# A decoder layer's FFN with its inner features on partitions from the first product on, and its layernorm taken through the second product from running sums

## The chip, the cores and the metric

The kernel runs on one core of a Trainium2 chip. The core has five engines with queues of their own: TensorE (PE in the profile; its weight loads, PEld, are listed apart), VectorE (DVE), ScalarE (ACT), GpSimd (POOL) and SyncE (SP, which here only issues DMAs). The metric is the device time of one execution in microseconds (us), of which several runs of a kernel are taken and the median is quoted.

## The reference

One pre-norm decoder layer over x of shape (4, 1024, 256): self-attention with 16 heads, cross-attention over 64 context tokens, and an FFN. Only the FFN is changed:

```python
m, v = mean(x, -1), var(x, -1)
xn = (x - m) / sqrt(v + 1e-5)                        # layernorm without weights, over 256
h = gelu(xn @ absmean(W_fc).T)                       # 256 -> 1024, exact gelu
mu, var = mean(h, -1), mean((h - mu) ** 2, -1)       # over the 1024 inner features
h = (h - mu) * rsqrt(var + 1e-5) * ln_w + ln_b
x = x + h @ absmean(W_proj).T                        # 1024 -> 256
```

absmean(W) turns a weight matrix into values of -1, 0 and 1. All data are float32.

## The kernel before

Tokens lie on partitions in tiles of 128; E = 256, HID = 1024, NT = 8 tiles to a batch, B = 4 batches. The long first stage (the loop `for u in range(NU)`, L891) runs the self-attention of all batches, and between its steps the projections and the rest (`post`, L540: output projection, cross-attention) of the batch before. The helper `fill` (L694) places that work; a third line of work, `aside`, takes the last batch's spare places for `ternary` (L722, absmean of the two weight matrices) and `bias_row` (L760). `bias_row` makes `yrow`, the row ln_b @ W_proj, on TensorE as plain float32, in the four 32-column strips that `product` uses in this stage.

After the loop the pools are closed and new ones opened (L962 to L971): PSUM as `wide`, two tiles of two banks each, and `misc`, four tiles of one bank each. What follows I call the last stage. It runs the FFN of all 32 token tiles, and beside it the generator `last`, which is `post` of batch 3.

The FFN works on eight halves of a batch (NH = 4 tiles, 512 tokens). `widen(i)` (L976) does for half i: `ln_normalised` and `ln_transposed` of two tiles at a time (four TensorE transposes into one bank; ACT casts to `xh`, DVE makes the rest `xl`, both in the float32r format), `add_row` of `yrow` on POOL (L280), then per tile 8 matmuls of 512 columns with weights `xl`/`xh` and moving `wfc` into a `wide` tile; the gelu over 1024 columns goes to `h` with the tokens on partitions (L1001), DVE takes its statistics (L1004, L1005). When all four tiles are there, `ln_rstd` takes a square root on ACT and a reciprocal on DVE, and `h` is normalised in place, two tiles on DVE (L1012), two on ACT (L1015).

`narrow(i)` (L1020) takes the 8 chunks of 128 inner features: four transposes of `h` into one `misc` bank, ACT scales by `lnw` and rounds to `hT` (L1035), DVE makes the rest `hl` (L1036), and two chunks later 8 matmuls of 256 columns add into `py`, a `wide` tile. At the end DVE adds `py` to x (L1052) and SP issues two stores.

PE instructions and the DMAs on SP keep the order in which the program issues them. The order of the last stage is written out by hand: `widen` and `narrow` of each half are generators with a place number for every step (`WIDE`, `NARROW`, L1077, 16 numbers to a half), the generator with the lowest next number steps, and two of every five turns go to `last` (L1085). `narrow(i)` begins only when `widen(i)` is done, and a step of gelus isn't taken while `last` is between its exponentials (L1095).

Of the kernel before, what the change touches and what calls it, by code (L numbers as in the profile page):

```python
# [10 lines left out]
F32R = mybir.dt.float32r  # L11
DRAM = bass.MemoryType.DRAM
# [8 lines left out]
HID = 1024  # L21
# [9 lines left out]
def decoder_layer(ctx, tc, a, out):  # L31
# [204 lines left out]
    def ln_rstd(pool, rs, mv):  # L236
        n = mv.shape[1]
        sd = pool.tile([P, n], F32, tag="sd", name="sd", bufs=2)
        nc.scalar.activation(sd, mv[:, :, 1], AF.Sqrt, bias=eps_t[:, 0:1])
        nc.vector.reciprocal(out=rs, in_=sd)  # L240

# [478 lines left out]
    yrow = const.tile([P, E], F32, name="yrow")  # L720

# [37 lines left out]

    def bias_row():  # L760

        yield "free"
        wide = main.tile([P, HID // P, P], F32, tag="hl", name="lnb_wide", bufs=2)
        nc.gpsimd.tensor_copy(
            wide, late["lnb"].rearrange("p (c o) -> p c o", o=1).to_broadcast([P, HID // P, P])
        )
        yield "cols"
        pt = bank()
        w = ternaries[1].bitcast(F32)
        product(pt[:, 0:E], [(wide[:, c, :], w[:, c, :]) for c in range(HID // P)])  # L770
        nc.vector.tensor_copy(yrow, pt[:, 0:E])
# [119 lines left out]
    for u in range(NU):  # L891
# [23 lines left out]
        if g == 1 and b == B - 1:  # L915
            aside.add(ternary("wfc", 2, HID), 10)
            aside.add(ternary("wproj", HID // P, E), 10)
            aside.add(bias_row(), 2)
# [54 lines left out]
    h_of = {}  # L973
    NH = NT // 2

    def widen(i):  # L976
# [10 lines left out]
        h = ffn.tile([P, NH, HID], F32, tag="h", name="h", bufs=2)  # L987
        mv = ffn.tile([P, NH, 2], F32, tag="mvh", name="mvh", bufs=2)
        rs = ffn.tile([P, NH], F32, tag="rsh", name="rsh", bufs=2)
        h_of[i] = h  # L990
        for t in range(NH):
            yield "Gelu"
            ph = ps["wide"]()
            for half in range(2):
                for k in range(4):
                    c, part = divmod(k, 2)
                    matmul(
                        ph[:, half, :], lhsT=(xl, xh)[part][:, c, t * P : (t + 1) * P],
                        rhs=wfc[:, c, half * 512 : (half + 1) * 512], start=k == 0, stop=k == 3,
                    )  # L1000
            nc.scalar.activation(h[:, t, :], ph.rearrange("p a f -> p (a f)"), AF.Gelu)  # L1001
            st = ffn.tile([P, 2, 6], F32, tag="bnh", name="bnh", bufs=3)
            for half in range(2):
                nc.vector.bn_stats(out=st[:, half, :], in_=h[:, t, half * 512 : (half + 1) * 512])  # L1004
            nc.vector.bn_aggr(out=mv[:, t, :], in_=st)  # L1005
        yield "Sqrt"
        ln_rstd(ffn, rs, mv)
        nmr = ffn.tile([P, NH], F32, tag="nmr", name="nmr", bufs=2)
        nc.vector.scalar_tensor_tensor(nmr, mv[:, :, 0], -1.0, rs, ALU.mult, ALU.mult)
        for t in range(0, NH, 2):  # L1010
            yield ""
            nc.vector.tensor_scalar(  # L1012
                h[:, t, :], h[:, t, :], mv[:, t, 0:1], rs[:, t : t + 1], ALU.subtract, ALU.mult
            )
            nc.scalar.activation(  # L1015
                h[:, t + 1, :], h[:, t + 1, :], AF.Identity, bias=nmr[:, t + 1 : t + 2],
                scale=rs[:, t + 1 : t + 2],
            )

    def narrow(i):  # L1020


        h = h_of.pop(i)
        t0 = i * NH
        py = ps["wide"]()
        parts = []
        for c in range(HID // P + 2):
            if c < HID // P:
                pt = bank()
                for n in range(NH):  # L1030
                    transpose(pt[:, n * P : (n + 1) * P], h[:, n, c * P : (c + 1) * P], ident)
                hT = ffn.tile([P, 512], F32R, tag="hT", name="hT", bufs=4)
                hl = ffn.tile([P, 512], F32R, tag="hl", name="hl", bufs=4)
                w = late["lnw"][:, c : c + 1]
                nc.scalar.activation(hT, pt, AF.Copy, scale=w)  # L1035
                nc.vector.scalar_tensor_tensor(hl, pt, w, hT.bitcast(F32), ALU.mult, ALU.subtract)  # L1036
# [127 lines left out]
```

## Time and profile before

Three runs gave 1364.13, 1367.08 and 1367.55 us, median 1367.08. The profiled execution took 1365.17 us, of which its span is 1363.4 us.

| stretch of the span | us | PE busy | DVE busy | ACT busy | POOL busy |
|---|---|---|---|---|---|
| to the end of the attention loop, 0 to 1101.6 | 1101.6 | 1048.7 | 834.9 | 741.0 | 53.9 |
| FFN with post of batch 3, 1101.6 to 1298.4 | 196.8 | 178.6 | 130.7 | 122.5 | 23.5 |
| FFN alone, one half to the next, 1298.4 to 1322.8 | 24.4 | 21.5 | 17.0 | 16.3 | 2.7 |
| to the end, 1322.8 to 1363.4 | 40.6 | 33.3 | 22.2 | 18.7 | 0.0 |

Busy times are from the profile's table by stretches. A busy PE is not a PE at its peak: the matmuls overlap, so what a group of them costs is read from one start to the next. The groups of instructions give for each line, engine and operation the output and inputs by the program's names, the shape, the count, the total and the mean in ns; "ps_misc<-ident,h" are the transposes of `h`, "ps_wide<-wfc,xl" matmuls of the first product, "ps_wide<-wproj,hl" of the second.

### The profile page before, as it was taken

How to read it: one execution, taken by the hardware profiler on the slowest of the kernel's cores; microseconds unless marked ns; L12 is line 12 of the kernel's file. 1: busy time of each engine (PE TensorE's matmuls, PEld its weight loads, DVE VectorE, ACT ScalarE, POOL GpSimd, SP SyncE). 2: the span in 40 equal slices, each digit the busy share in tenths (PEclk: the TensorE clock that was granted, in tenths of full speed). 3: DMA queues.
4: the chain of work that ended last, by engine and by line, in shares of the span. 5: the costliest groups of instructions: out<-in, count | busy, mean ns of one | idle time of the engine just before them, and what ended most of it. 6: DMA issues, size and time to landing. Idle time of an engine off the chain costs nothing.

```text
span 1363.4 us, 27651 instructions
## 1 busy us (share of the span) xinstructions
PE 1282.1 (94%) x11000; PEld 717.4 (53%) x11000; DVE 1004.7 (74%) x2110; ACT 898.5 (66%) x1654; POOL 80.0 (6%) x86
## 2 busy tenths in 40 slices
PE   3879999999999999999999999999999988999987
PEld 1434445545545454444545544545455466776777
DVE  4877777867878877877877777878889357565665
ACT  1377666756687667777676676676766746474765
POOL 4000000003010000011000000010000012000000
PEclk9889999999999999989999999999999989999989
DMA  5440312312130202131212112212210010100000
GB/s 169 126 143 30 111 42 68 94 48 63 41 85 1 63 7 57 33 93 31 64 35 60 38 27 75 82 53 73 55 40 1 2 62 1 44 19 31 1 31 32
DMA packets 46064, 72.72 MB, mean 53 GB/s; under 512 B 11280, under 2 KB 27920, under 8 KB 45936
## 3 DMA queue, kind: packets, MB, share of 16 engines
q1 hardware_dynamic: 44720, 68.47, 17.0%
q8 instruction: 87, 1.43, 0.4%
q10 hardware_dynamic: 1072, 2.10, 0.4%
q0 software_dynamic: 144, 0.39, 0.2%
q14 instruction: 41, 0.34, 0.1%
HBM read 46.81 MB, written 24.12 MB: 52 GB/s over the span
## 4 chain that ended last, share of the span: by engine, by line
PE 73%; DVE 16%; ACT 8%; issue 2%; DMA 1%; SPq 0%; DVEq 0%; ACTq 0%
PE ps_ring L57 42%; PE ps_acc L57 15%; PE ps_wide L57 8%; DVE mx L433 8%; PE ps_misc L57 3%; ACT exp L888 3%; PE ps_misc L60 2%; PE ps_ring L60 2%; DVE nm L592 2%; ACT xn L250 1%; DVE xn L256 1%; DVE bn L233 1%; DMA x<-in_x 1%; ACT ex L625 1%; ACT hl L359 1%
## 5 line engine op out<-in xcount | busy, mean ns | idle before, releaser
L433 DVE TENSOR_REDUCE mx<-ps_ring 128x1 f32<-128x512 f32 x1024 | 646.4, 682 | 157.6 <-PE ps_ring L57 156.7
L888 ACT ACTIVATE exp<-ps_ring 128x512 f32<-128x512 f32 x1024 | 549.2, 606 | 191.1 <-PE ps_ring L57 187.5
L57 PE MATMUL ps_ring<-q,k 64*128 64x512 f32 x1024 | 280.5, 474 | 8.0 <-ACT exp L888 5.9
L57 PE MATMUL ps_ring<-k,q 64*128 64x512 f32 x1024 | 260.2, 425 | 20.1 <-DMA q<-kept_q 7.9
L57 PE MATMUL ps_acc<-exp,v_sb 128*32 128x512 f32 x2048 | 275.3, 610 | 0.0
L57 PE MATMUL ps_ring<-mT,sel 64*128 64x512 f32 x1024 | 232.8, 400 | 0.2 <-ACT mT L451 0.2
L57 PEld LDWEIGHTS ps_ring<-q,k 64*128 64x128 f32 x1024 | 115.5, 185 | 198.4 <-ACT exp L888 69.0
L57 PEld LDWEIGHTS ps_ring<-k,q 64*128 64x128 f32 x1024 | 124.2, 186 | 100.2 <-ACT exp L888 41.3
L57 PEld LDWEIGHTS ps_ring<-mT,sel 64*128 64x128 f32 x1024 | 108.0, 186 | 6.3 <-ACT mT L451 0.7
L57 PEld LDWEIGHTS ps_acc<-exp,v_sb 128*32 128x32 f32 x2048 | 40.5, 108 | 67.4 <-issue 65.6
L1004 DVE BATCH_NORM_STATS2 bnh<-h 128x6 f32<-128x512 f32 x64 | 41.2, 679 | 34.1 <-ACT h L1001 34.0
L1001 ACT ACTIVATE h<-ps_wide 128x1024 f32<-128x1024 f32 x32 | 32.7, 1026 | 41.6 <-PE ps_wide L57 41.5
L1036 DVE SCALAR_TENSOR_TENSOR hl<-ps_misc,lnw,hT 128x512 fp32r<-128x512 f32 x64 | 46.4, 733 | 18.2 <-ACT hT L1035 18.2
L57 PE MATMUL ps_wide<-wproj,hl 128*128 128x256 f32 x256 | 46.2, 303 | 12.6 <-DVE hl L1036 12.5
L57 PE MATMUL ps_wide<-wfc,xl 128*128 128x512 f32 x128 | 56.5, 442 | 1.4 <-DVE xl L271 1.4
L57 PE MATMUL ps_wide<-wfc,xh 128*128 128x512 f32 x128 | 54.3, 424 | 0.0
L1035 ACT ACTIVATE hT<-ps_misc,lnw 128x512 fp32r<-128x512 f32 x64 | 42.6, 687 | 16.3 <-PE ps_misc L60 16.3
L233 DVE BATCH_NORM_STATS2 bn<-x 128x6 f32<-128x256 f32 x96 | 38.8, 416 | 8.1 <-DMA x<-in_x 6.4
L57 PEld LDWEIGHTS ps_wide<-wproj,hl 128*128 128x128 f32 x256 | 34.9, 191 | 16.2 <-DVE hl L1036 14.8
L280 POOL TENSOR_TENSOR x<-x,xbo 128x512 f32<-128x512 f32 x16 | 20.6, 1295 | 367.0 <-ACT xn L250 358.5
L57 PE MATMUL ps_wide<-wproj,hT 128*128 128x256 f32 x256 | 41.4, 284 | 0.0
L407 ACT COPY v_sb<-ps_ring 128x256 f32<-128x256 f32 x32 | 12.0, 375 | 41.0 <-PE ps_ring L57 30.6
(166 smaller groups left out, 1467.1 us busy)
## 6 DMA issues: line engine op xcount, KB each, us to landing
k<-kept_k SPq DMA_DIRECT2D x248, 64.0 KB
q<-kept_q SPq DMA_DIRECT2D x240, 64.0 KB
kept_q<-hl SPq DMA_DIRECT2D x15, 512.0 KB
kept_k<-hl SPq DMA_DIRECT2D x14, 512.0 KB
out<-x SPq DMA_DIRECT2D x16, 256.0 KB
x<-in_x SPq DMA_DIRECT2D x3, 1024.0 KB
x_kept<-x SPq DMA_DIRECT2D x3, 1024.0 KB
x<-x_kept SPq DMA_DIRECT2D x3, 1024.0 KB
```

Of the source, the lines that this page charges most:

```text
L57: ordered(nc.tensor.matmul(*args, **kwargs))
L60: ordered(nc.tensor.transpose(*args))
L233: nc.vector.bn_stats(out=st, in_=xs(t)[:, 0, :])
L250: nc.scalar.activation(xn[:, k, :], xs(t + k)[:, 0, :], AF.Identity, bias=nmr[:, k : k + 1], scale=rs[:, i + k : i + k + 1],)
L280: nc.gpsimd.tensor_tensor(xs(t, 2), xs(t, 2), row.rearrange("p (o d) -> p o d", o=1).to_broadcast([P, 2, E]), ALU.add,)
L433: nc.vector.tensor_reduce(mx[:, t, 2 * pair + n : 2 * pair + n + 1, kh], pm, AX.X, ALU.max)
L592: nc.vector.tensor_reduce(nm[:, t, s, :], pm[s].rearrange("p (h k) -> p h k", k=SK), AX.X, ALU.max, negate=True,)
L888: nc.scalar.activation(ex[:, n, :], pe[n], AF.Exp)
L1001: nc.scalar.activation(h[:, t, :], ph.rearrange("p a f -> p (a f)"), AF.Gelu)
L1004: nc.vector.bn_stats(out=st[:, half, :], in_=h[:, t, half * 512 : (half + 1) * 512])
L1035: nc.scalar.activation(hT, pt, AF.Copy, scale=w)
L1036: nc.vector.scalar_tensor_tensor(hl, pt, w, hT.bitcast(F32), ALU.mult, ALU.subtract)
```

## The change

The first product is turned round: `wfc` becomes the stationary operand and xh/xl the moving one, so that a PSUM bank holds 128 inner features of 512 tokens. Per chunk c of 8, ACT takes the gelu into `h`, scales `h` by `lnw` into `hT` and squares `h` into `sq`; DVE makes `hl` from `h` and `hT` and adds `h` to a running sum; POOL adds `sq` to a second running sum. The transposes of `h`, its statistics, its square root and its normalisation in place go.

After chunk 7 the two sums are transposed on TensorE (8 transposes), reduced on DVE to mean and mean square of each token, and POOL works out 1/sqrt(var + eps) by `ln_root`: a first value from the bits, three Newton steps. In these and the four operations ahead of it are 21 small POOL operations of 128x4.

The second product works on the h that is scaled by `lnw` but neither shifted nor normalised. `narrow` has no transposes; it adds to x, in steps c = 3 and 5, `crow` times -mean/std (`crow` is the row lnw @ W_proj), and at the end `py` times 1/std. `yrow` and `crow` are made at the start of the last stage, with 16 float32r matmuls each, whose stationary operand is a column of `lnb` or `lnw` repeated 128 times; `bias_row` goes from the attention loop.

The first product's banks come from `misc` now, `wide` serves `py` alone, `h` has four buffers of one chunk, `sq` three, `hT` and `hl` ten each. The places of the steps and the share of turns for `last` are new: 7 steps of `widen`, 8 of `narrow`, and four of every nine turns.

```diff
+    def ln_root(pool, rs, mv):
+        n = mv.shape[1]
+        by = pool.tile([P, 4, n], F32, tag="root", name="root", bufs=2)
+        var, half, t, nmr = (by[:, i, :] for i in range(4))
+        engine = nc.gpsimd
+        engine.tensor_scalar(var, mv[:, :, 1], 0.0, LN_EPS, ALU.max, ALU.add)
+        engine.tensor_scalar(half, var, -0.5, None, ALU.mult)
+        engine.tensor_scalar(
+            rs.bitcast(I32), var.bitcast(I32), -0.5, float(0x5F3759DF), ALU.mult, ALU.add
+        )
+        for _ in range(3):
+            engine.tensor_tensor(t, rs, half, ALU.mult)
+            engine.tensor_tensor(t, t, rs, ALU.mult)
+            engine.tensor_scalar(t, t, 1.5, None, ALU.add)
+            engine.tensor_tensor(rs, rs, t, ALU.mult)
+        engine.tensor_tensor(nmr, mv[:, :, 0], rs, ALU.mult)
+        engine.tensor_scalar(nmr, nmr, -1.0, None, ALU.mult)
+        return nmr
...
-            aside.add(bias_row(), 2)
...
-        h = ffn.tile([P, NH, HID], F32, tag="h", name="h", bufs=2)
+        h_of[i] = deque()
+        sums = ffn.tile([P, 2, 512], F32, tag="sums", name="sums", bufs=2)
+        last = None
+        for c in range(HID // P):
+            if c % 2 == 0:
+                yield "Gelu"
+            ph = bank()
+            for k in range(4):
+                f, part = divmod(k, 2)
+                matmul(
+                    ph, lhsT=wfc[:, f, c * P : (c + 1) * P], rhs=(xl, xh)[part][:, f, :],
+                    start=k == 0, stop=k == 3,
+                )
+            h = ffn.tile([P, 512], F32, tag="h", name="h", bufs=4)
+            sq = ffn.tile([P, 512], F32, tag="sq", name="sq", bufs=3)
+            hT, hl = (ffn.tile([P, 512], F32R, tag=tag, name=tag, bufs=10) for tag in ("hT", "hl"))
+            h_of[i].append((hl, hT))
+            nc.scalar.activation(h, ph, AF.Gelu)
+            w = late["lnw"][:, c : c + 1]
+            nc.scalar.activation(hT, h, AF.Copy, scale=w)
+            nc.scalar.activation(sq, h, AF.Square)
+            nc.vector.scalar_tensor_tensor(
+                hl, h, w, hT.bitcast(F32), ALU.mult, ALU.subtract
+            )
+            if last is not None:
+                before = last if c == 1 else (sums[:, 0, :], sums[:, 1, :])
+                nc.vector.tensor_tensor(sums[:, 0, :], before[0], h, ALU.add)
+                nc.gpsimd.tensor_tensor(sums[:, 1, :], before[1], sq, ALU.add)
+            last = h, sq
+        yield ""
         mv = ffn.tile([P, NH, 2], F32, tag="mvh", name="mvh", bufs=2)
         rs = ffn.tile([P, NH], F32, tag="rsh", name="rsh", bufs=2)
-        h_of[i] = h
-        for t in range(NH):
-            yield "Gelu"
-            ph = ps["wide"]()
-            for half in range(2):
-                for k in range(4):
-                    c, part = divmod(k, 2)
-                    matmul(
-                        ph[:, half, :], lhsT=(xl, xh)[part][:, c, t * P : (t + 1) * P],
-                        rhs=wfc[:, c, half * 512 : (half + 1) * 512], start=k == 0, stop=k == 3,
-                    )
-            nc.scalar.activation(h[:, t, :], ph.rearrange("p a f -> p (a f)"), AF.Gelu)
-            st = ffn.tile([P, 2, 6], F32, tag="bnh", name="bnh", bufs=3)
-            for half in range(2):
-                nc.vector.bn_stats(out=st[:, half, :], in_=h[:, t, half * 512 : (half + 1) * 512])
-            nc.vector.bn_aggr(out=mv[:, t, :], in_=st)
-        yield "Sqrt"
-        ln_rstd(ffn, rs, mv)
-        nmr = ffn.tile([P, NH], F32, tag="nmr", name="nmr", bufs=2)
-        nc.vector.scalar_tensor_tensor(nmr, mv[:, :, 0], -1.0, rs, ALU.mult, ALU.mult)
-        for t in range(0, NH, 2):
-            yield ""
-            nc.vector.tensor_scalar(
-                h[:, t, :], h[:, t, :], mv[:, t, 0:1], rs[:, t : t + 1], ALU.subtract, ALU.mult
-            )
-            nc.scalar.activation(
-                h[:, t + 1, :], h[:, t + 1, :], AF.Identity, bias=nmr[:, t + 1 : t + 2],
-                scale=rs[:, t + 1 : t + 2],
-            )
+        total = ffn.tile([P, 3, NH], F32, tag="total", name="total", bufs=2)
+        for k in range(2):
+            pt = bank()
+            for n in range(NH):
+                transpose(pt[:, n * P : (n + 1) * P], sums[:, k, n * P : (n + 1) * P], ident)
+            nc.vector.tensor_reduce(
+                total[:, k, :], pt.rearrange("p (n k) -> p n k", n=NH), AX.X, ALU.add
+            )
+        mean, square = mv[:, :, 0], total[:, 2, :]
+        nc.gpsimd.tensor_scalar(mean, total[:, 0, :], 1.0 / HID, None, ALU.mult)
+        nc.gpsimd.tensor_tensor(square, mean, mean, ALU.mult)
+        nc.gpsimd.tensor_scalar(mv[:, :, 1], total[:, 1, :], 1.0 / HID, None, ALU.mult)
+        nc.gpsimd.tensor_tensor(mv[:, :, 1], mv[:, :, 1], square, ALU.subtract)
+        shift_of[i] = rs, ln_root(ffn, rs, mv)
 
     def narrow(i):
-        h = h_of.pop(i)
+        parts = h_of.pop(i)
+        rs, nmr = shift_of.pop(i)
         t0 = i * NH
         py = ps["wide"]()
-        parts = []
-        for c in range(HID // P + 2):
-            if c < HID // P:
-                pt = bank()
+        for c in range(HID // P):
+            if c:
+                yield ""
+            for k, part in enumerate(parts.popleft()):
                 for n in range(NH):
-                    transpose(pt[:, n * P : (n + 1) * P], h[:, n, c * P : (c + 1) * P], ident)
-                hT = ffn.tile([P, 512], F32R, tag="hT", name="hT", bufs=4)
-                hl = ffn.tile([P, 512], F32R, tag="hl", name="hl", bufs=4)
-                w = late["lnw"][:, c : c + 1]
-                nc.scalar.activation(hT, pt, AF.Copy, scale=w)
-                nc.vector.scalar_tensor_tensor(hl, pt, w, hT.bitcast(F32), ALU.mult, ALU.subtract)
-                parts.append((hl, hT))
-            if c >= 2:
-                for k, part in enumerate(parts[c - 2]):
-                    for n in range(NH):
-                        matmul(
-                            py[:, n // 2, n % 2 * E : (n % 2 + 1) * E], lhsT=part[:, n * P : (n + 1) * P],
-                            rhs=wproj[:, c - 2, :], start=c == 2 and k == 0 and n % 2 == 0,
-                            stop=c == HID // P + 1 and k == 1 and n % 2 == 1,
-                        )
-            if 0 < c < HID // P + 1:
-                yield ""
-        for n in range(2):
-            rows = xs(t0 + 2 * n, 2)
-            nc.vector.tensor_tensor(
-                rows, rows, py[:, n, :].rearrange("p (n d) -> p n d", n=2), ALU.add
-            )
-            dma(out=out_view[:, t0 + 2 * n : t0 + 2 * n + 2, :], in_=rows)
+                    matmul(
+                        py[:, n // 2, n % 2 * E : (n % 2 + 1) * E],
+                        lhsT=part[:, n * P : (n + 1) * P], rhs=wproj[:, c, :],
+                        start=c == 0 and k == 0 and n % 2 == 0,
+                        stop=c == HID // P - 1 and k == 1 and n % 2 == 1,
+                    )
+            if c in (3, 5):
+                for n in range(c - 3, c - 1):
+                    row = xs(t0 + n)[:, 0, :]
+                    nc.vector.scalar_tensor_tensor(
+                        row, crow, nmr[:, n : n + 1], row, ALU.mult, ALU.add
+                    )
+        for n in range(NH):
+            row = xs(t0 + n)[:, 0, :]
+            nc.vector.scalar_tensor_tensor(
+                row, py[:, n // 2, n % 2 * E : (n % 2 + 1) * E], rs[:, n : n + 1], row, ALU.mult,
+                ALU.add,
+            )
+            if n % 2:
+                dma(out=out_view[:, t0 + n - 1 : t0 + n + 1, :], in_=xs(t0 + n - 1, 2))
         if i == 1:
             load_x(2, view=x_kept, slot=1)
+    yrow, crow = (ffn.tile([P, E], F32, name=name) for name in ("yrow", "crow"))
+    for row, name in ((yrow, "lnb"), (crow, "lnw")):
+        two = ffn.tile([P, 2, HID // P], F32R, name=f"{name}_parts")
+        nc.vector.tensor_copy(two[:, 0, :], late[name])
+        nc.vector.tensor_tensor(two[:, 1, :], late[name], two[:, 0, :].bitcast(F32), ALU.subtract)
+        pt = bank()
+        for c in range(HID // P):
+            for k in range(2):
+                matmul(
+                    pt[:, 0:E], lhsT=two[:, k, c : c + 1].to_broadcast([P, P]), rhs=wproj[:, c, :],
+                    start=c == 0 and k == 0, stop=c == HID // P - 1 and k == 1,
+                )
+        nc.vector.tensor_copy(row, pt[:, 0:E])
...
-    WIDE, NARROW = (-6, -4, 0, 1, 3, 7, 8, 10, 12), (2, 4, 5, 6, 9, 11, 13, 14, 15)
+    WIDE, NARROW = (-4, -2, 1, 4, 7, 10, 13), (0, 2, 3, 5, 6, 8, 9, 11)
-        if tag is not None and turn % 5 in (0, 2):
+        if tag is not None and turn % 9 in (0, 2, 4, 6):
...
-            apart = exps % NG and tag is not None and wides[0].tag in ("Gelu", "Sqrt")
+            apart = exps % NG and tag is not None and wides[0].tag == "Gelu"
```

More of the change, by code (lines that the diff above doesn't have):

```diff
@@ L11 @@
 F32R = mybir.dt.float32r
+I32 = mybir.dt.int32
 DRAM = bass.MemoryType.DRAM
@@ L718, in decoder_layer @@
     ternaries = []
-    yrow = const.tile([P, E], F32, name="yrow")
     def ternary(name, *shape):
@@ L758, in ternary @@
             )
[L760 to L765, printed above, removed]
-        )
-        yield "cols"
-        pt = bank()
-        w = ternaries[1].bitcast(F32)
-        product(pt[:, 0:E], [(wide[:, c, :], w[:, c, :]) for c in range(HID // P)])
-        nc.vector.tensor_copy(yrow, pt[:, 0:E])
     def run(gen):
@@ L972, in decoder_layer @@
     out_view = out.rearrange("(t p) d -> p t d", p=P)
-    h_of = {}
+    h_of, shift_of = {}, {}
     NH = NT // 2
@@ L1020, in narrow @@
+        nc.gpsimd.tensor_scalar(mv[:, :, 1], total[:, 1, :], 1.0 / HID, None, ALU.mult)
+        nc.gpsimd.tensor_tensor(mv[:, :, 1], mv[:, :, 1], square, ALU.subtract)
+        shift_of[i] = rs, ln_root(ffn, rs, mv)
     def narrow(i):
-        h = h_of.pop(i)
+        parts = h_of.pop(i)
+        rs, nmr = shift_of.pop(i)
         t0 = i * NH
         py = ps["wide"]()
-        parts = []
-        for c in range(HID // P + 2):
-            if c < HID // P:
-                pt = bank()
+        for c in range(HID // P):
+            if c:
+                yield ""
+            for k, part in enumerate(parts.popleft()):
```

## The prediction

> **What bounds the kernel now.** I read the page first, then the chain of waits, then the instructions in order of time in the last stage.
>
> ```profile
> PE 1282.1 (94%) x11000; PEld 717.4 (53%) x11000; DVE 1004.7 (74%) x2110; ACT 898.5 (66%) x1654; POOL 80.0 (6%) x86
> ```
>
> TensorE is busy nearly all the span, POOL hardly ever. The change touches the last stage, 262 us from 1101.6 on, and one piece ahead of it. The chain there shows what one half costs when nothing runs beside the FFN (start, us, what; pieces left out are more of the same):
>
> ```profile
> 1298.45 6.47 PE ps_wide L57 x24
> 1304.92 0.87 PE ps_misc L60 x8
> ...
> 1315.33 0.45 PE ps_misc L60 x4
> 1315.81 0.69 ACT hT L1035
> 1316.52 1.28 ACT L239
> 1318.11 0.48 ACT xh L269
> 1318.58 2.34 ACT h L1015 x2
> 1320.92 0.47 ACT xh L269
> 1321.42 0.69 DVE xl L271
> 1322.12 0.67 DVE hl L1036
> 1322.83 6.47 PE ps_wide L57 x24
> ```
>
> The reader is to see a period of 24.4 us: 17.3 us of pure TensorE, then 7.0 us in which it waits for a table load, the square root, the normalisation and the next half's operands. So two things bound a half: PE's own work and the layernorm in its middle.
>
> **TensorE.** Costs are from start to start. Eight matmuls of the first product take 1.87 us (1336.30 to 1338.17), so 32 take 7.5. One chunk of `narrow` with its four transposes takes 1.39 (1333.52 to 1334.91); four transposes in the chain take 0.44, so 8 matmuls take 0.95. A half costs now 7.5 + 8 x 1.39 + 0.9 (transposes of `xn`) = 19.5 us. After: 7.5 + 7.6 + 0.9 + 0.9 (transposes of the sums) = 16.9. The turned first product has as many matmuls and loads. That is 2.6 us less a half, 21 us in all. Also, the 24 matmuls after each 7 us gap take 6.47 instead of 24 x 0.234 = 5.6: they start 0.43 apart at first, at a lower clock. With a shorter gap some of this 0.85 us a half goes.
>
> **ScalarE.** Now per half: gelus 4 x 1.03, `hT` 8 x 0.62, normalisation 2.36, `xh` 1.2, the root 0.3, table loads (22 of 1.283 us by L1001 and L239) 3.5: 16.4. After: gelu and `sq` at 0.52 each (as `exp`, four in 2.07), `hT` 0.62, so 8 x 1.66 + 1.2 = 14.5. **Square** has no row. The Trainium skill (ScalarE: Activation LUTs, Table sets) says that cheap functions such as copy and identity sit in every table set; it doesn't name square there. The trace shows `hT` copies between gelus without loads. By the row of the copy it costs no load; if it were outside the gelu's set, 128 loads x 1.283 = 164 us. I take none.
>
> **VectorE.** Now 147 us for the FFN in this stage, 18.4 a half. After: `hl` 8 x 0.70 (the nearest row with two SBUF inputs, L755: two in 1.40 at 964.61), sums 7 x 0.60, `xn` 4 x 0.37, `crow` 4 x 0.42, `py` 4 x 0.42, `xl` and the reductions 2.5: 17.2. Alone that is no loss.
>
> **POOL, and the rule that speaks against the change.** POOL goes from two adds a half to nine, and 21 small operations. An add of 512 takes 1.28; the smallest rows are 0.10 (memset) and 0.24 (copy of 64), so the small ones take 2 to 5 us. `sq` adds take 7 x 1.28 = 9 of a period: POOL alone isn't full. But it meets DVE:
>
> ```profile
> 1200.87 1.28 POOL L280 TENSOR_TENSOR x<-x,yrow 128x512 f32<-128x512 f32 x1 [2.27 <-DVE rsh L240]
> 1200.91 1.26 DVE L1009 SCALAR_TENSOR_TENSOR nmr<-mvh,rsh 128x4 f32<-128x4 f32 x1
> ```
>
> ```profile
> 1054.66 1.23 POOL L764 COPY lnb_wide<-lnb 128x1024 f32<-128x1024 f32 x1 [143.56 <-DVE wproj L755]
> 1055.03 1.41 DVE L755 SCALAR_TENSOR_TENSOR wproj<-raw,thr,neg 128x512 fp32r<-128x512 f32 x1
> ```
>
> A DVE operation of four elements (shortest 0.155) and one of 512 (0.744 elsewhere) both last until POOL is done: each reads two SBUF inputs. Four `xn` (DVE, 1289.41, 2.36 together instead of 1.46) met one POOL add: 0.9 us lost. `bn_stats`, with one input, ran on unharmed at 1197.17. The skill (SBUF — State Buffer, Who interferes with whom) calls the port pair of the two an exclusive lock, held for the full instruction, taken by a DVE operation with two SBUF inputs or in a two-port mode. Now `hl` reads PSUM and is free of it; after, `hl`, sums, `xn` and `crow` all need the lock: 5.6 + 4.2 + 1.5 + 1.7 = 13.0 us a half. POOL's nine adds hold it 9 x 1.28 = 11.5 by the rule, 9 x 0.9 = 8.1 by the row; the small ones 1 to 2. Sum 26 by the rule, 22.5 by the row, which I take. In a chunk that is 0.70 + 0.60 + 0.9 = 2.2 us, more than PE's 1.9 and ACT's 1.66. **The lock is late next**, not PE.
>
> **The stage between halves.** The table load, the root and the normalisation (3.9 us of the 7.0) and the wait for `hl` go. New waits stand in PE's queue: the transposes of the sums wait for the last `hl`, sum and `sq` add of chunk 7 (gelu, copy, square 1.7 behind chunk 6's, then POOL 1.28), covered by one chunk of `narrow`, 0.95. Behind them stand the next half's transposes. From the last add to the next half's first `hl`: transposes 1.4, `xh` 0.6, two `xl` 1.3 (one behind the reductions), four matmuls 0.94, gelu and copy 1.1: 5.3 us, in which POOL's small operations and `yrow` adds find room. On ACT the square waits for one of three `sq` buffers, so for POOL; the next gelus are queued behind it, and a full bank behind those stops PE.
>
> **FFN alone to the end** (now 65.0 us from 1298.4). One period: 5.3 + 8 x 2.2 + 1.7 (`crow`) + 0.8 lost = 25.4, against 24.4. The last `widen`: 8 x 2.2 + 1.7 + 0.2 = 19.5, against 20.1. Then `narrow` of the last half: wait and transposes 2, 8 x 0.95 = 7.6, `py` 1.7, the stores 4.1 as now: 15.4 against 20.5, since its transposes, `hT` and `hl` are gone. Sum 60.3: -5 us.
>
> **FFN with post** (now 196.8 us, about 5.4 halves). PE saves 5.4 x 2.6 = 14 us at most if it bounds all of it. DVE, 130.7 busy now, gets 5.4 x (17.2 + 8.1 - 18.4) = 37 us of work and blocking: 168, or 85%; PE falls from 91% to 83%. Two engines at that share and queues in order: bounds -19 (with less of the slow clock) and +12 (a third of DVE's 37 not hidden). I take -4.
>
> **bias_row, yrow, crow.** Its 64 small matmuls (1097.15, 3.64 us) stand on PE just before the last attention products. They go; but DVE's `rs` comes at 1099.87, its first `xn` at 1101.85, so 2.0 is gained rather than 3.6. The 32 new matmuls take 32 x 0.12 = 3.8 us, at the lower clock up to 7.6; PE idles some 3.5 us between 1102 and 1107.4. I take +2, so 0 together, bounds -3 and +4. DMAs and SP's order stay.
>
> **Sum:** -5 - 4 + 0 = -9. The profiled execution took 1365.2, so 1356; the median of the runs lies 1.9 above it, so **1358**. Its own range, with the bounds of the mixed stretch cut to those that go with it: 1343 to 1363.
>
> **Rivals.**
> 1. *The lock decides* (0.36). DVE and POOL never fill each other's gaps: every add costs DVE 0.9, and what stands behind a blocked DVE operation (`xl`, reductions, `py`) is late too. A half takes 5.3 + 17.6 + 1.7 + 1.7 (`py`) + 1.8 (`yrow` adds) = 28.1, 3.7 more than now; eight halves +29, less 5 for the end: 1391. It decides once lock and DVE together pass 24.4 us a half; the rows put them at 22.5 to 26.8. For it: the L755 and L1009 rows. Against it: post's work fills gaps in five of eight halves.
> 2. *PE stays the bound* (0.10): POOL fits beside DVE. A half alone takes 16.9 + 3 = 20; 2.65 halves save 12, the end 3, the mixed stretch 19: 1333. For it: DVE at 66% now.
> 3. *No change* (0.12): the transposes saved only make PE wait longer for DVE: 1367, give or take 4.
> 4. *Square outside the set* (0.02): the change wouldn't do what it says, 1450 or more.
>
> **Numbers.** Forecast 0.40. Of it 0.02 falls within 0.3%, about 4 us, which is what runs can tell apart here. Faster 0.38 + 0.10 = 0.48; same 0.14; slower 0.36 + 0.02 = 0.38. As both signs hold much, the range goes from near rival 2 to rival 1's price: 1337 to 1392.
>
> **What would show it.** PE: no `ident,h` rows, 64 transposes of sums, steady period near 25. Lock: `hl` and sums well over 0.7, `sq` adds over 1.3, where their times overlap; with means near 0.7 and 1.28 rival 2 is right. ACT: loads down from 22 to a handful; many would show rival 4. Waits of PE for the sums should be near 2 to 3 us a half. The forecast is wrong if the mixed stretch lengthens, which only the lock or the smaller buffers could do.

## The result and the profile after

The changed kernel takes 1416.15 us (median of 4 runs, 1414.97 to 1416.88), the kernel before 1366.38 in the same comparison (4 runs, 1364.13 to 1367.55): a ratio of 1.0365, with a 95% interval of 1.0350 to 1.0379. That is 50 us slower, and outside the range of the prediction. The profiled execution of the changed kernel has a span of 1415.0 us.

The page of the changed kernel, first part (busy time, share, instructions), and the rows of the FFN's main groups in its fifth part (busy us and mean ns of one; then idle time of the engine just before them, and what ended it):

```profile
PE 1272.5 (90%) x10776; PEld 709.1 (50%) x10776; DVE 1068.6 (76%) x2107; ACT 898.1 (63%) x1713; POOL 201.3 (14%) x309
...
L1021 POOL TENSOR_TENSOR sums<-sums,sq 128x512 f32<-128x512 f32 x48 | 72.5, 1510 | 68.6 <-ACT sq L1014 66.4
L1015 DVE SCALAR_TENSOR_TENSOR hl<-h,lnw,hT 128x512 fp32r<-128x512 f32 x64 | 77.0, 1212 | 4.4 <-ACT hT L1013 4.0
...
L1020 DVE TENSOR_TENSOR sums<-sums,h 128x512 f32<-128x512 f32 x48 | 55.5, 1157 | 15.2 <-ACT h L1011 14.4
...
L61 PE MATMUL ps_misc<-ident,sums 128*128 128x128 f32 x64 | 14.4, 391 | 48.8 <-DVE sums L1020 48.2
```

PE has 224 instructions fewer and is 9.6 us less busy, as the change says. But `hl`, costed at 0.70, takes 1.21; the sums, costed at 0.60, take 1.16; and PE stands 48 us in front of the transposes of the sums, some 7 us at each of seven of them, where I had written 2 to 3. The page gives the sums of waits; how one comes about is seen in the instructions in order of time. Here are DVE's in one half late in the changed kernel, when post's work is over and nothing but the FFN runs (start, duration, engine, line, what; in brackets the idle time before and what ended it):

```profile
1351.88 2.70 DVE L1065 SCALAR_TENSOR_TENSOR x<-crow,root,x 128x256 f32<-128x256 f32 x4 [2.42 <-POOL root L262]
1354.50 0.74 DVE L1015 SCALAR_TENSOR_TENSOR hl<-h,lnw,hT 128x512 fp32r<-128x512 f32 x1
...
1357.79 1.78 DVE L1020 TENSOR_TENSOR sums<-sums,h 128x512 f32<-128x512 f32 x1
1359.50 1.78 DVE L1015 SCALAR_TENSOR_TENSOR hl<-h,lnw,hT 128x512 fp32r<-128x512 f32 x1
1361.20 1.78 DVE L1020 TENSOR_TENSOR sums<-sums,h 128x512 f32<-128x512 f32 x1
1362.90 1.75 DVE L1015 SCALAR_TENSOR_TENSOR hl<-h,lnw,hT 128x512 fp32r<-128x512 f32 x1
...
1369.59 0.74 DVE L1015 SCALAR_TENSOR_TENSOR hl<-h,lnw,hT 128x512 fp32r<-128x512 f32 x1
1370.25 0.68 DVE L1020 TENSOR_TENSOR sums<-sums,h 128x512 f32<-128x512 f32 x1
```

and POOL's in the same time:

```profile
1359.10 10.01 POOL L1021 TENSOR_TENSOR sums<-sums,sq 128x512 f32<-128x512 f32 x6
```

From 1357.79 on, DVE starts an instruction every 1.67 to 1.71 us and POOL one every 1.67: they take turns, one DVE operation to one POOL addition. When POOL is done (1369.11), the same two DVE operations start 0.66 and 0.60 apart. So each addition of squares delays one DVE operation by 1.0 to 1.1 us. That is what the `lnb_wide` and `L1009` lines of before had shown once each, now as a steady state. (ACT, whose square waits for POOL when its three buffers are full, stood for that only twice in the last stage, 4.8 us in all.)

PE in that half, the transposes of the sums of two halves, one after the other (the same view):

```profile
1343.51 1.94 PE L61 MATMUL ps_misc<-ident,sums 128*128 128x128 f32 x8 [10.35 <-DVE sums L1020]
1372.64 1.97 PE L61 MATMUL ps_misc<-ident,sums 128*128 128x128 f32 x8 [9.73 <-DVE sums L1020]
```

The period is 29.1 us (the next one 27.1, up to 1399.71), against 24.4 before. PE had done all the products that it could do by 1362.9 and stands for 9.7 us until DVE has worked off `hl` and sums. And the first of DVE's lines shows a second thing: DVE stands 2.42 us at the `crow` additions until POOL has finished the root, with the `hl` of the next half behind them in its queue.

The waits over the whole last stage of the changed kernel (total us, times, longest):

```profile
PE ps_misc L61 <- DVE sums L1020: 48.2, 7, 10.3
...
DVE x L1065 <- POOL root L262: 20.0, 7, 5.6
```

**Where the time went.** The last attention product starts at 1101.0 before and at 1096.5 after, so the stage starts 4.5 us sooner. Only 2.5 of that is `bias_row`: from the start of the loop's last `xwo` product (1094.8 and 1092.8) to that of the last attention product it is 6.2 us before and 3.7 after. The other 2.0 came earlier; in the profiles without `bias_row` that `xwo` product starts anywhere from 1090.7 to 1095.7.

To compare the rest, the stage is best cut where the same FFN work is left. Post's last product is no such place: 80 of the first product's 256 matmuls stand behind it before, 96 after, as the places of the steps are new. With 64 of them left, the first products of the last two halves, post's products are over in both kernels; the first of the 64 starts at 1299.5 before and at 1348.6 after. From the end of the last attention product (1101.6 and 1097.1) to there it is 197.9 us before and 251.5 after: 53.6 more. From there to the end it is 63.9 and 66.4: 2.5 more, the net of two longer halves and a shorter last `narrow`. So 53.6 + 2.5 - 4.5 makes the 51.6 us by which the spans differ, and nearly all of it lies beside post's work, not in the half that can be read so well above.

### The profile page after: what moved, and what is told of

Same layout as the page of the kernel before. It is cut to its first block, busy times and chain, and to the rows that moved or that the text cites. A ratio compares the mean times of both kernels' runs of the same rounds, so it can differ in the third digit from the quotient of the medians.

```text
span 1415.0 us, 27592 instructions
## 1 busy us (share of the span) xinstructions
PE 1272.5 (90%) x10776; PEld 709.1 (50%) x10776; DVE 1068.6 (76%) x2107; ACT 898.1 (63%) x1713; POOL 201.3 (14%) x309
## 4 chain that ended last, share of the span: by engine, by line
PE 65%; DVE 19%; ACT 8%; issue 5%; DMA 2%; POOL 1%; SPq 0%; DVEq 0%; POOLq 0%; ACTq 0%
PE ps_ring L58 41%; PE ps_acc L58 15%; DVE mx L456 7%; PE ps_misc L58 4%; DVE sums L1020 3%; ACT exp L896 3%; PE ps_ring L61 2%; DVE nm L615 2%; DVE hl L1015 2%; PE ps_wide L58 1%; DMA x<-in_x 1%; PE ps_misc L61 1%; DVE xn L279 1%; ACT xn L273 1%; ACT h L1011 1%
## 5 line engine op out<-in xcount | busy, mean ns | idle before, releaser
L1021 POOL TENSOR_TENSOR sums<-sums,sq 128x512 f32<-128x512 f32 x48 | 72.5, 1510 | 68.6 <-ACT sq L1014 66.4
L1015 DVE SCALAR_TENSOR_TENSOR hl<-h,lnw,hT 128x512 fp32r<-128x512 f32 x64 | 77.0, 1212 | 4.4 <-ACT hT L1013 4.0
L1020 DVE TENSOR_TENSOR sums<-sums,h 128x512 f32<-128x512 f32 x48 | 55.5, 1157 | 15.2 <-ACT h L1011 14.4
L1011 ACT ACTIVATE h<-ps_misc 128x512 f32<-128x512 f32 x64 | 36.8, 592 | 34.1 <-PE ps_misc L58 29.2
L61 PE MATMUL ps_misc<-ident,sums 128*128 128x128 f32 x64 | 14.4, 391 | 48.8 <-DVE sums L1020 48.2
L58 PE MATMUL ps_misc<-xl,wfc 128*128 128x512 f32 x128 | 53.4, 417 | 2.3 <-DVE xl L294 2.3
L303 POOL TENSOR_TENSOR x<-x,bo 128x512 f32<-128x512 f32 x16 | 20.1, 1297 | 239.3 <-ACT xn L273 209.8
L303 POOL TENSOR_TENSOR x<-x,yrow 128x512 f32<-128x512 f32 x16 | 22.5, 1410 | 217.6 <-DVE yrow L1093 190.4
L58 PE MATMUL ps_misc<-xh,wfc 128*128 128x512 f32 x128 | 50.8, 397 | 0.0
L292 ACT CAST xh<-ps_misc 128x512 fp32r<-128x512 f32 x16 | 9.2, 587 | 60.6 <-PE ps_misc L61 60.5
```

The source lines that it names most:

```text
L58: ordered(nc.tensor.matmul(*args, **kwargs))
L61: ordered(nc.tensor.transpose(*args))
L303: nc.gpsimd.tensor_tensor(xs(t, 2), xs(t, 2), row.rearrange("p (o d) -> p o d", o=1).to_broadcast([P, 2, E]), ALU.add,)
L1011: nc.scalar.activation(h, ph, AF.Gelu)
L1015: nc.vector.scalar_tensor_tensor(hl, h, w, hT.bitcast(F32), ALU.mult, ALU.subtract)
L1020: nc.vector.tensor_tensor(sums[:, 0, :], before[0], h, ALU.add)
```

## The experiments

My theory after this reading: the shared port of DVE and POOL decides, beside post's work too. Rivals: the waits come from the order on PE's queue (the transposes of the sums, ahead of the next half's); from the `crow` additions in front of `hl`; from the scalar engine's squares, or from the smaller PSUM banks.

**e1. The additions of the squares taken away.** Against the changed kernel:

```diff
-                nc.gpsimd.tensor_tensor(sums[:, 1, :], before[1], sq, ALU.add)
+                if c == HID // P - 1:
+                    nc.gpsimd.tensor_tensor(sums[:, 1, :], last[1], sq, ALU.add)
```

> Leaves out six of the seven POOL adds of squares of each half (only the one at chunk 7 stays), so the variance is taken from two chunks alone; ACT still squares. Lock theory: hl falls from 1.21 to about 0.73 us and the sums from 1.16 to about 0.67, which frees DVE of some 55 us in the last stage, and the time falls by 40 to 50 us, to 1366 to 1376. Rival, the order on PE (the transposes of the sums wait in PE's queue for the end of a chain of gelu, copy, sum whatever that chain's speed): PE's wait for the sums stays over 4 us a half and the time stays above 1395. Rival, DVE held by the wait for POOL's root: that wait stays at 2 to 5 us a half and the time stays above 1395.

Measured: 1384.49 us, ratio 1.0141 (1.0126 to 1.0157). Six of seven additions a half are worth 31 us, three fifths of the loss: less than the 40 to 50 that the lock alone was to give, and below the 1395 of both rivals. The page's rows of the two DVE operations in e1:

```profile
L1015 DVE SCALAR_TENSOR_TENSOR hl<-h,lnw,hT 128x512 fp32r<-128x512 f32 x64 | 51.3, 808 | 5.6 <-ACT hT L1013 4.9
...
L1020 DVE TENSOR_TENSOR sums<-sums,h 128x512 f32<-128x512 f32 x48 | 33.8, 704 | 20.7 <-ACT h L1011 19.9
```

Their means fall from 1212 and 1157 to 808 and 704, PE's wait for DVE's sums from 48.2 to 15.6 us, and the stretch with the last two halves from 66.4 to 54.5, which is 9.4 less than before the change. The lock is shown; but the kernel is still 1.4% slower than before.

**e2. The additions on DVE in place of POOL** (`nc.gpsimd` to `nc.vector` in the same line).

> The seven adds of squares of each half go from POOL to DVE, all else as in the change. Lock theory: every one of the blocked DVE operations gets its 1.0 us back while DVE gains 56 adds of 0.6 us (34 us), so DVE has about 25 us less to do in the last stage and the time falls to 1385 to 1400; hl and sums last 0.66 to 0.75 us. Order theory and root theory: DVE's queue is as long or longer, the time stays at 1410 to 1430.

Measured: 1403.93 us, 1.0281 (1.0260 to 1.0302), between the two cases and nearer to the lock's. The rows in e2:

```profile
L1015 DVE SCALAR_TENSOR_TENSOR hl<-h,lnw,hT 128x512 fp32r<-128x512 f32 x64 | 51.1, 799 | 4.5 <-ACT hT L1013 4.1
L1021 DVE TENSOR_TENSOR sums<-sums,sq 128x512 f32<-128x512 f32 x48 | 32.7, 682 | 0.0
```

The additions are all still made, and `hl` is short again: it was POOL beside it that made it long. The same work on the fuller engine is 12 us faster than on the emptier one: an addition takes DVE 0.68, but costs it 1.0 or more when POOL does it.

**e3. The totals later on PE.** The transposes of the sums and the root moved, as a function `totals`, from the end of `widen` into `narrow`, behind its third chunk; the `crow` additions at chunks 5 and 7:

```diff
+            if c == 2:
+                totals(i)
+                rs, nmr = shift_of.pop(i)
-            if c in (3, 5):
-                for n in range(c - 3, c - 1):
+            if c in (5, 7):
+                for n in range(c - 5, c - 3):
```

> The transposes of the sums, the reductions and POOL's root move from the end of widen into narrow, behind its third chunk, so that PE's queue has the next half's transposes and three chunks of narrow ahead of them; crow is added at chunks 5 and 7. The POOL adds stay. Order theory: PE's waits for the sums (75 us with its weight loads) nearly go and the time falls by 40 us or more, to below 1376. Lock theory: DVE and POOL stay full at about 27 us a half, PE waits elsewhere, and the time falls by 5 to 20 us only; hl and sums stay above 1.1 us.

Measured: 1411.91 us, 1.0344 (1.0327 to 1.0361), some 3 to 4 us less. PE's wait has mostly changed its name. In e3 PE now waits for the next operands from the same late DVE:

```profile
DVE x L1069 <- POOL root L262: 38.2, 8, 6.1
PE ps_misc L58 <- DVE xl L294: 35.1, 6, 12.8
```

The edit also puts DVE 38.2 us before the root, where it was 20.0, so e3 alone does not price the order on PE's queue. With e1, in which that order stands and the wait for DVE's sums falls to a third, the order falls as the main cause.

**e4. The `crow` additions alone two chunks later** (the last four lines of e3's diff).

> Only crow's four additions of a half move, from chunks 3 and 5 to chunks 5 and 7, so that DVE doesn't stand at them until POOL's root is done. Root theory (DVE idle 20 us in front of crow, with hl and the sums queued behind): the time falls by 12 to 20 us, to 1396 to 1404. Lock theory: DVE takes up the freed time with blocked operations, the time falls by 0 to 8 us.

Measured: 1416.02 us, 1.0379 (1.0355 to 1.0404): no gain. The wait of DVE for the root is 20.0 us as before the edit, because the instructions stand in DVE's queue where they stood; moving them in the program didn't move them there. So e4 says nothing of what that wait costs; e8 to e12 do.

**e5. No squares at all:** neither `Square` on ACT nor its additions.

```diff
-            sq = ffn.tile([P, 512], F32, tag="sq", name="sq", bufs=3)
-            nc.scalar.activation(sq, h, AF.Square)
-                nc.gpsimd.tensor_tensor(sums[:, 1, :], before[1], sq, ALU.add)
```

> Leaves out the squares on ACT and every add of squares (the transposes and reductions of the second sum read the first), so no POOL add of a chunk and 64 ACT operations of 0.62 us less than the change. ACT theory for what is left once the lock is gone (the first run stood 19 us above the kernel before; the FFN's ACT work now comes in bursts of 1.66 us a chunk inside the gelu steps, with post's small ACT operations and the sums queued behind): 10 to 20 us below the first run, 1365 to 1375. Rival, the four misc banks or the share of turns: no more than 5 us below it, 1380 to 1385.

Measured: 1365.34 us, 0.9993 (0.9983 to 1.0003), the time of before. Against e1, 64 squares on ACT and the last addition are worth another 20 us. No run parts the two: in e1 PE also stood 8.4 us for that last addition on POOL. The squares take 39.9 us of ACT (623 ns each) on an engine that is busy less than two thirds of the span. The chain of waits between 1096 and 1305 us shows how they can come to count. By line, in e1:

```profile
by line: PE ps_misc L58 29.7%; PE ps_wide L58 8.2%; ACT sq L1014 7.7%; ACT h L1011 7.1%; ACT hT L1013 6.4%; issue 6.4%; PE ps_misc L61 5.6%; DVE xn L279 4.3%; POOL sums L1022 3.0%; ACT ex L648 2.0%; ACT L1011 1.8%; DVE x L1066 1.7%; ACT L64
```

and in e5:

```profile
by line: PE ps_misc L58 35.4%; PE ps_wide L58 14.5%; DVE sums L1018 6.4%; issue 6.1%; DVE hl L1013 6.1%; PE ps_misc L61 5.1%; DVE xn L279 2.6%; ACT h L1010 2.0%; DVE xl L294 1.8%; ACT hT L1012 1.6%; DVE x L1067 1.5%; DVE nm L615 1.4%; DVE t
```

With squares, gelu, copy and square hold 21% of the chain, without them gelu and copy 4%. One piece of e1's chain in order of time shows the form of it:

```profile
1181.28 1.28 ACT L1011
1182.57 1.09 ACT h L1011 x2
1183.66 0.60 ACT hT L1013
1184.27 0.52 ACT sq L1014
1184.79 0.61 ACT hT L1013
1185.39 0.52 ACT sq L1014
1185.92 1.28 ACT L648
1187.21 0.60 ACT ex L648
1187.86 1.05 PE ps_misc L58 x4
```

A table load for the gelu, two gelus, two copies, two squares, a table load back, and only then post's `ex`, for which PE waits. A square isn't filler there: each stands in front of post's short operations in an in-order queue. Post's last product comes at 1305.9 in e1 and at 1287.3 in e5, 18.6 us apart (the program's order is the same in both), so nearly all of it falls beside post.

**e6. The same with other PSUM banks** (`misc` six, `wide` one, in place of four and two).

> As the run without squares, and the PSUM banks dealt out anew: six misc banks of one and a single wide tile, since the first product now takes its banks from misc. Bank theory: 8 us or more below the run without squares. ACT theory: within 4 us of it, or slower by some us because narrow of the next half must wait for the one wide tile.

Measured: 1365.67 us, 0.9995 (0.9983 to 1.0007), against 0.9993 for e5. Two banks more for the first product gain nothing there. (They are taken from `wide`, so a gain and a loss could cancel.)

**e7. The fold alone.** The kernel before, tokens on partitions and `bn_stats` as they were; only the layernorm goes through the second product, and `yrow` and `crow` are made as in the change. Its core, against the kernel before:

```diff
-        for t in range(0, NH, 2):
-            yield ""
-            nc.vector.tensor_scalar(
-                h[:, t, :], h[:, t, :], mv[:, t, 0:1], rs[:, t : t + 1], ALU.subtract, ALU.mult
-            )
...
+        shift_of[i] = rs, nmr
...
+            if c in (5, 7):
+                for n in range(c - 5, c - 3):
+                    row = xs(t0 + n)[:, 0, :]
+                    nc.vector.scalar_tensor_tensor(
+                        row, crow, nmr[:, n : n + 1], row, ALU.mult, ALU.add
+                    )
...
+        for n in range(NH):
+            row = xs(t0 + n)[:, 0, :]
+            nc.vector.scalar_tensor_tensor(
+                row, py[:, n // 2, n % 2 * E : (n % 2 + 1) * E], rs[:, n : n + 1], row, ALU.mult,
+                ALU.add,
+            )
```

> The second half of the change alone, in the kernel before: tokens stay on partitions in the first product, with bn_stats, the square root on ACT and the transposes of h, but h isn't normalised; narrow takes the raw h and the normalisation is taken through the second product (crow, and py times 1/std). No running sums, no squares, no POOL adds beyond yrow's. If what costs is the layout with its sums (lock and ACT bursts): the normalisation (2.4 us ACT, 1.5 us DVE a half) and the wait for it in the middle of a half go, and the time is 10 to 30 us below the kernel before, 1335 to 1356. If taking the layernorm through the product costs by itself (crow's and py's additions, the wait for the root): 1370 or more.

Measured: 1364.20 us, 0.9981 (0.9968 to 0.9993): 2 to 3 us faster than before, and in neither of the two cases expected. The part of the change that needs no sums and no squares is sound, and small as it stands here. The order has changed with it, though: `widen` has two steps less while the share of turns for post is the same, so post's last product now has only 64 of the first product's matmuls behind it, where 80 were before. What the fold would give with turns dealt anew was not tried.

**e8. The fold with the change's root on POOL** (`ln_rstd` in e7 replaced by `ln_root`).

> As the run before this one, with the square root on ACT and its table loads replaced by POOL's 21 small operations. If table loads matter: 5 to 12 us below that run. If POOL's small operations get in DVE's way or the root comes late: above it.

Measured: 1389.00 us, 1.0168 (1.0146 to 1.0190), 25 us slower than e7, from 17 operations of four elements a half (not 21: `bn_stats` gives mean and variance here). In e8 the waits name them:

```profile
DVE x L1048 <- POOL root L262: 31.2, 8, 5.6
PEld ps_wide L58 <- DVE hl L1033: 23.2, 10, 4.9
PE ps_wide L58 <- DVE hl L1033: 20.1, 9, 4.6
```

On all eight halves DVE stands at its `crow` additions until POOL is done; behind them in DVE's queue is `hl`, and PE waits for `hl`. This can be read as DVE standing in its queue or as the length of the root; the next run tells these apart.

**e9. e8 with the root on DVE:**

```diff
-        engine = nc.gpsimd
+        engine = nc.vector
```

> The kernel before with the layernorm taken through the second product, and the same Newton root, with its 17 small operations issued on DVE in place of POOL (no Sqrt on ACT, so no table loads for it). If the 25 us by which the root on POOL was slower than the root on ACT are DVE standing in order at the crow additions until POOL is done, they go when DVE does the root itself: its own operations of four elements take about 0.16 to 0.18 each (rsh and nmr rows of before), some 17 x 0.2 = 3.4 a half, no longer than the wait they replace, with no handover on either side, so 1366 to 1378. If on the other hand it is the length of the root (a half's second product can't be completed before it), it stays near 1389. If the table loads taken out of ACT count for something, it comes below 1364.

Measured: 1361.62 us, 0.9963 (0.9948 to 0.9977). All of the 25 us go, and it comes below the expected 1366 to 1378, where the table loads were to count. The root is as many operations, now ahead of the `crow` additions on their own engine, and no wait of DVE for it is left. PE's waits for `hl`, 20.1 and 23.2 us in e8, are in e9:

```profile
PEld ps_wide L58 <- DVE hl L1033: 11.9, 11, 3.8
...
PE ps_wide L58 <- DVE hl L1033: 8.6, 7, 3.6
```

From its first operation to its last the root is not much shorter: 4.9 us in the last two halves of e8 (1340.45 to 1345.33 in one), 4.2 and 5.4 in those of e9 (1322.25 to 1326.40 in one), with other DVE work in between. So it is not its length that cost 25 us, but that DVE stood while POOL worked. In the trace of e9 one of these operations lasts 0.16 where nothing stands beside it (POOL: 0.20), and its last stage has 12 table loads where e7 has 25. Of the kernels that compute the whole it is the fastest, 5 us under the kernel before, with none of the change's turned first product in it. (Against e7 alone the intervals overlap: 0.9963, up to 0.9977, and 0.9981, from 0.9968.)

**e10. The change with the small operations on DVE** (the same line, and the four operations of mean and variance; the squares' additions stay on POOL).

> The change, with mean, variance and root (21 small operations a half) issued on DVE in place of POOL; the additions of the squares stay on POOL. The waits of DVE for the root (20 us in the change) go, DVE gets about 21 x 0.2 = 4.2 us a half of its own, and those that fall beside an addition of squares last until that is done, since they read two SBUF inputs. If the wait for the root is a term of its own, 1396 to 1410; if the shared port and the squares on ACT hide it, 1412 to 1420 or above.

Measured: 1410.13 us, 1.0321 (1.0304 to 1.0338): 6 us less, at the upper edge of the first case. With the lock still there the root counts for little; the rows in e10 are close to those of the change:

```profile
L1021 POOL TENSOR_TENSOR sums<-sums,sq 128x512 f32<-128x512 f32 x48 | 73.0, 1521 | 70.0 <-ACT sq L1014 68.0
L1015 DVE SCALAR_TENSOR_TENSOR hl<-h,lnw,hT 128x512 fp32r<-128x512 f32 x64 | 71.4, 1123 | 2.1 <-ACT hT L1013 1.7
```

**e11. e5 with the small operations on DVE.**

> The change without the squares (neither the Square on ACT nor their additions on POOL; the second total reads the first sum, so the variance is not computed) and with the small operations on DVE. What is left of the change is the turned first product, the sums, their transposes and the fold. Without the squares the change takes 1365, as long as before, with PE's work 21 us less and 27 us of DVE waiting for the root. If that wait is what keeps the 21 us from showing, 1342 to 1355; if DVE and ACT in the gelu steps bound it, 1360 to 1370.

Measured: 1357.20 us, 0.9933 (0.9918 to 0.9948): 8 us under e5, 9 under before, a little outside the 1342 to 1355 of the first theory. So the wait for the root is a term of its own there, but it isn't all that hides PE's 21 us: PE still waits 16 us for the sums.

**e12. The squares' additions and the small operations on DVE.**

> The change with both the additions of squares and the small operations on DVE: POOL keeps only the additions of yrow. Against the squares on DVE alone (1404) the handover of the root goes and DVE gets some 4 us a half. If the handover is a term of its own, 1385 to 1397; if DVE's own amount of work bounds the half by then, 1400 to 1412.

Measured: 1388.81 us, 1.0161 (1.0146 to 1.0177): 15 us under e2 and within the first case. It is the change's whole computation with POOL out of the way: 27 us of the 50 are back.

**The sum.** Taken off one after the other, by ratio times 1366 us: additions of squares on POOL 31 (1.0365 to 1.0141), squares on ACT and the last addition 20 (to 0.9993), the root on POOL 8 (to 0.9933), and what is left of the change, without its variance, is 9 faster than before. The order matters: the root is worth 6 while the lock is there (e10) and 15 beside additions on DVE (e12).

The same by stretches of equal FFN work (us):

| kernel | from the last attention product to the last two halves' first products | from there to the end |
|---|---|---|
| before | 197.9 | 63.9 |
| after | 251.5 | 66.4 |
| e1 | 231.3 | 54.5 |
| e5 | 211.8 | 53.9 |
| e11 | 206.4 | 51.9 |
| e9 | 210.6 | 50.6 |

The gain is at the end, 12 us in e11. Beside post, even e11 is 8.5 us slower than before, and e9, with neither sums nor squares, 12.7. What holds these is open. The order of the steps differs from before in all these kernels, and no run changed it alone (e3 takes one step out along with its edit), so the new order is a rival that stands untested for them.

## Why the prediction was wrong

It gave 1358 us, with the fold and the saved transposes 9 us ahead. A gain of that size shows in e11, at 0.9933, but only with the squares left out and the root off POOL. The costs beside it were mis-sized, and most of the miss is in one term, the stretch with post.

- **"FFN with post ... I take -4"** is the step that failed. The bounds were -19 and +12; measured to the place with the same work left it is +53.6, less the 4.5 us by which the stage starts sooner. I had counted DVE's and POOL's shares of busy time (85%, PE 83%) and let nearly all of it hide. e1 puts 20 us of this on the lock, e5 another 19.5 on the squares and the last addition, e11 some 5 on the root on POOL; 8.5 stay open. A longer mixed stretch was the prediction's own sign of being wrong, but it allowed only the lock or smaller buffers as the reason: the queues of ACT and DVE were not in it.
- **"ScalarE: 16.4 before, 14.5 after".** ACT was to have 1.9 us less a half, 15 in all; it is as busy as it was (898.5 us before, 898.1 after). A chunk takes it 1.76 to 1.78 us from start to start where 1.66 was put (gelus at 1359.59, 1361.36, 1363.12, 1364.88). The inference that a square needs no load held: 25 table loads from 1095 us on before, 12 after. The conclusion didn't. I entered ACT as freed; the squares stand in bursts between two gelus, ahead of post's operations. No case of mine priced ACT beside post.
- **The junction, "5.3 us ... in which POOL's small operations ... find room".** From the transposes of the sums to the next half's first `hl` it is 11.0 us (1343.51 to 1354.50) and 10.1 (1372.64 to 1382.77). I had put the reductions in front of `xl`, but not asked who is queued behind an instruction that waits for the root: `crow` on DVE, with `hl` behind it. In the first of the two ACT had the first `hT` ready at 1351.14, so 3.4 of the 5.7 us too many are that queue. The small operations' own time was near (2 to 5 us estimated, 6 measured: 21 at 0.28 to 0.30 from start to start); that DVE stands through it was left out.
- **The lock by the row, 0.9 us an addition.** Right in kind, and close in size: 1.0 to 1.1. The eight chunks were put at 17.6 us and take 18.1 (1354.50 to 1372.6). The Trainium skill (SBUF — State Buffer, Who interferes with whom) says the pair is held for the full instruction, 1.28 here; the trace agrees that one engine blocks the other entirely, but the price seen is a little under that. "The lock is late next, not PE" held. What I didn't do is carry it into the stretch with post.
- **The end, -5.** With the same work left it is 2.5 us longer, not 5 shorter. The last `narrow` came as put: 15.3 us from the transposes of its sums (1399.71) to the end, for 15.4. The two halves ahead of it did not: 51.1 us (1348.56 to 1399.71) for 25.4 and 19.5. With the lock gone (e1) the end is 9.4 shorter.
- **PE's waits for the sums, "2 to 3 us a half, covered by one chunk of narrow"**: 48.2 us over seven, up to 10.3. Most of it follows from the lock: in e1 they fall to 15.6, so 2.2 each, with 8.4 more for the one addition left on POOL.
- **`bias_row`, `yrow`, `crow`: 0.** Its going gained 2.5 us, for 2.0, and the 32 products, 3.9 us in the trace, are in the stage: near.
- **A misread row.** The 24 matmuls of 6.47 us after each gap were priced at 0.234 each. At 1298.45 eight of them are of 256 columns, at 0.12 each, so at the spacing of the later ones the 24 take 4.7 us and not 5.6: the slow start costs 1.8 us a half, where 0.85 was put.

Rival 1, the lock, was the right one of the four, with its period (28.1 us put, 29.1 and 27.1 measured), and its 1391 was 25 too low: it charged each half beside post the 3.7 us of a half alone, where it lost some 9 (53.6 us over six halves), since the squares and the root were priced at nothing there.

## What to carry to other kernels

Before moving work to an idle engine, ask what it shares with the full one: here an addition on POOL cost DVE more than doing it on DVE. When a small calculation is handed to another engine, look at the instruction that waits for the result and at everything queued behind it; on the waiting engine itself the same 17 operations a half made the kernel 27 us faster (e8 and e9). And a stretch in which two pieces of work are interleaved is not priced by shares of busy time: list, for each in-order queue, what now stands in front of the other piece's short operations.

## What the runs showed of the hardware

- DVE and POOL, both with two-input operations on SBUF in steady supply, alternate strictly, one to one, at 1.67 to 1.71 us a turn, against 0.60 to 0.66 for the DVE operation alone and 1.28 for the POOL addition as I had it from before. Both lose.
- The granted TensorE clock is lower here where PE has more gaps. The same stretch of three kernels by windows (busy time of PE, PEld, DVE, ACT and POOL with their instructions; then the clock): the kernel before, the changed kernel, and e5, in this order.

```profile
1102.00:1306.00 204.00, 186.14 (x1106) 143.59 (x1107) 135.00 (x284) 125.95 (x165) 26.14 (x20) 0.96 0.07 24
```

```profile
1102.00:1306.00 204.00, 157.57 (x821) 113.03 (x819) 141.57 (x216) 107.49 (x180) 90.54 (x134) 0.88 0.06 18
```

```profile
1102.00:1306.00 204.00, 172.64 (x976) 130.64 (x976) 137.19 (x262) 102.52 (x163) 48.71 (x123) 0.95 0.06 19
```

With PE busy 91%, 77% and 85% of the time, the clock is 0.96, 0.88 and 0.95 (e1: 81% and 0.89). So waits may cost more than their own length; how much of the 50 us is this wasn't separated.
